# Block 0's norms on VectorE through PSUM, a GELU bias as a row of ones, a split MLP front, and heads-of-eight attention in finer parts

## The chip, the cores and the metric

One core of a Trainium2 chip. The kernel is one launch, and its time is device microseconds, the median of several runs. Engines: TensorE (PE, its weight loads PEld), VectorE (DVE), ScalarE (ACT), GpSimd (POOL), and SyncE (SP), which issues most DMAs. Each runs its own queue in order, and semaphores join them.

## What is computed

X is 16 batches of 128 tokens of 128 features, f32. Four blocks follow each other, each a gated cross-attention to a context of 77 rows and a gated feed-forward part. Blocks 0 and 2 begin with attention of 16 heads of width 8 ("heads of eight"). The feed-forward part of block 0 is itself six layers of local attention and a GELU MLP. Cut to what matters here:

```python
x = x + tanh(g_xattn[0]) * L0_xattn(layernorm(x), ctx, ctx, W1, W2, 16)   # heads of eight
x = x + tanh(g_ffn[0]) * L0_ffn(layernorm(x), ...)                        # below
...                                                                       # blocks 1, 2 (heads of eight), 3

def L0_ffn(x):                       # DEPTH 6, 16 heads of 64
    for i in range(6):
        q, k, v = split(shift_tokens(x) @ Wqkv[i])
        q, k = l2norm(q) * q_scale, l2norm(k) * k_scale    # t / max(norm, 1e-12)
        q, k = rotary(q), rotary(k)                        # with scales
        p = softmax(mask(8 * q @ k.T))                     # window of 32 and the one before
        x = (p @ v) @ Wo[i] + x
        xn = layernorm(shift_tokens(x)) * g + b
        a, gate = split(xn @ W1[i] + b1)                   # 341 + 341
        x = (a * gelu(gate)) @ W2[i] + b2 + x
```

shift_tokens moves the second half of the features by one token.

## The kernel before

X and, in block 0, Y stay in SBUF as four groups of four batches (GB 4), tokens on partitions. The order of the instructions on each engine is not the source's: the Tile framework's scheduler orders each engine's queue at build time from its own costs, keeps the data dependences, and sets the semaphores; an engine then runs its queue strictly in that order.

**Heads of eight** (`AttentionOf8`, used by `l0_xattn` and `l2_xattn`). A batch is a unit. `run` steps over n: scores of unit n (matmul L244, bias add on DVE L246, max on DVE L251, subtract on POOL L252, exp on ACT L253), row sums, reciprocal and division of unit n-1 (DVE L257, L258, POOL L259), transposes of unit n-2 (L266, copies on ACT L267), p times v of n-3 (L273, copied to oT by DVE, L275), output projection and gated add (L194) of n-4. For every four units `group` makes keys, layernorm (statistics and application on DVE, L179 to L183, power on POOL L171), transposes and queries in one go. The pool of `ps_s` has one buffer.

**Block 0's feed-forward part** (`l0_ffn`). A unit is one batch in one layer, worked in two halves of 8 heads; step k takes one half each of several units: `l0_project` (qk matmuls L454, two rotary multiplies of 128x1024 on DVE L457, squares on ACT L462, sums on DVE L463, rotary adds on POOL L466) and `l0_values` of half unit k; `l0_turn` (transposes of r, helper line L189) and `l0_scores` (mask matmul L505, scores L509, max on DVE L512, eight exps with row sums on ACT L516, reciprocal L517, division of p on POOL L518) of half unit k-3; `l0_turn_p` and `l0_mix` (L532, copy oT on ACT L534) of k-5; `l0_add` (ps_r L540, add to Y on DVE L541) of k-7. After a unit's second half, `l0_norms` makes the roots of the 32 norms of q and k:

```python
nc.scalar.activation(y, ss.bitcast(I32), AF.Exp, bias=seed, ...)   # L483: first guess
for c in (1.0 + 1.67e-4, 1.0):                                     # two Newton steps, L485 to L488, on POOL
```

and POOL multiplies r by them (L492). PSUM holds a pool "s" of two double banks (ps_qk, ps_s, ps_h) and a pool "m" of four banks for everything else. Two steps, an odd and an even one, make a pair; a half layer (8 units, two groups) is 8 pairs.

The MLP of a pair of groups hangs on fixed steps of this loop: `l0_mlp_norm` at step `at` (shift matmul ps_x L547, copies to xs, bn statistics on DVE, rs on POOL L557 to L560, adding b2 to Y on POOL L561 from the broadcast tile w_b2, four Identity activations on ACT L563), `l0_mlp_turn` at at+2, `l0_mlp_out` at at+3 and at+5 (ps_h L576 in three chunks, GELU on ACT L578, product on DVE L579 into h, w_2 matmuls L583, add to Y L584).

## Time and profile before

| | |
|---|---|
| median of 3 runs | 3260.86 us (3258.79 to 3262.26) |
| profiled execution | 3258.67 us, span 3256.9 us |
| granted TensorE clock, mean | 0.915 |
| PE busy in the span | 2756.5 us |
| first attention (heads of eight) | about 5 to 168 us |
| block 0's feed-forward part | about 168 to 2235 us |
| third block's attention (heads of eight) | about 2537 to 2700 us |

A line of a group reads: line, engine, operation, output tile <- input tiles, shapes, count, busy us, mean ns of one, idle us of the engine just before it and what ended it. A wait line reads: engine, tile and line that waited, what released it, total us, times, longest. A timeline line reads: start us, duration us, engine, line, operation, with the idle time before it in brackets. A window line: window, length, busy us and instructions of PE, PEld, DVE, ACT and POOL, granted clock, DMA share, GB/s.

### The profile page before, as it was taken

How to read it: one execution, taken by the hardware profiler on the slowest of the kernel's cores; microseconds unless marked ns; L12 is line 12 of the kernel's file. 1: busy time of each engine (PE TensorE's matmuls, PEld its weight loads, DVE VectorE, ACT ScalarE, POOL GpSimd, SP SyncE). 2: the span in 40 equal slices, each digit the busy share in tenths (PEclk: the TensorE clock that was granted, in tenths of full speed). 3: DMA queues.
4: the chain of work that ended last, by engine and by line, in shares of the span. 5: the costliest groups of instructions: out<-in, count | busy, mean ns of one | idle time of the engine just before them, and what ended most of it. 6: DMA issues, size and time to landing. Idle time of an engine off the chain costs nothing.

```text
span 3256.9 us, 50402 instructions
## 1 busy us (share of the span) xinstructions
PE 2756.5 (85%) x18912; PEld 1888.0 (58%) x18912; DVE 1876.6 (58%) x3163; ACT 1745.7 (54%) x5161; POOL 1778.9 (55%) x2030
## 2 busy tenths in 40 slices
PE   5779898989899898989898989898889678985656
PEld 4546565656566565656565656565655455653445
DVE  5566555555656564656565656545337765456553
ACT  3448676667667676758676767672222342222221
POOL 5568867686858585868776767751000451013222
PEclk8889999999999999999999999998779788997777
DMA  1020000000000000000000000002000000000003
GB/s 54 1 70 1 1 21 9 8 1 1 28 7 1 1 28 7 1 1 21 7 8 1 1 1 1 1 1 82 1 1 1 1 2 1 1 1 1 1 1 117
DMA packets 24304, 40.15 MB, mean 12 GB/s; under 512 B 1790, under 2 KB 18940, under 8 KB 22908
## 3 DMA queue, kind: packets, MB, share of 16 engines
q1 hardware_dynamic: 21036, 26.96, 2.5%
q0 software_dynamic: 2448, 9.07, 0.9%
q8 instruction: 149, 2.44, 0.3%
q10 hardware_dynamic: 576, 0.91, 0.1%
q14 instruction: 95, 0.78, 0.1%
HBM read 35.88 MB, written 1.05 MB: 11 GB/s over the span
## 4 chain that ended last, share of the span: by engine, by line
PE 46%; POOL 21%; ACT 15%; DVE 12%; issue 5%; DMA 1%; DVEq 0%; ACTq 0%; POOLq 0%
ACT p L516 7%; PE ps_t L189 7%; PE ps_qk L454 5%; POOL p L518 4%; POOL r L466 4%; PE ps_h L778 4%; POOL r L492 4%; PE ps_s L509 3%; PE ps_v L471 3%; DVE r L457 3%; PE ps_o L532 3%; PE ps_r L583 2%; PE ps_d L784 2%; PE ps_p L266 2%; PE ps_h L576 2%
## 5 line engine op out<-in xcount | busy, mean ns | idle before, releaser
L518 POOL TENSOR_TENSOR p<-p,rs 128x1024 f32<-128x1024 f32 x192 | 364.1, 1896 | 432.7 <-DVE rs L517 381.2
L516 ACT ACTIVATE p<-ps_s,mx 128x128 f32<-128x128 f32 x1536 | 539.6, 382 | 14.6 <-DVE mx L512 9.3
L457 DVE TENSOR_TENSOR r<-ps_qk,w_turn 128x1024 f32<-128x1024 f32 x384 | 454.2, 1215 | 140.2 <-PE ps_qk L454 74.8
L466 POOL TENSOR_TENSOR r<-r 128x512 f32<-128x512 f32 x384 | 480.7, 1271 | 9.5 <-DVE r L457 9.4
L454 PE MATMUL ps_qk<-w_qkv,xT 128*128 128x512 f32 x768 | 363.6, 596 | 5.3 <-ACT sq L462 3.3
L492 POOL TENSOR_TENSOR r<-r,nw_y 128x1024 f32<-128x1024 f32 x192 | 361.5, 1901 | 7.5
L516 ACT ACTIVATION_READ_ACCUMULATOR p<-ps_s,mx 128x1 f32 x1536 | 340.6, 222 | 0.0
L463 DVE TENSOR_REDUCE ss<-sq 128x16 f32<-128x1024 f32 x192 | 234.0, 1219 | 106.3 <-ACT sq L462 106.2
L189 PEld LDWEIGHTS ps_t<-const,p 128*128 128x128 f32 x1536 | 178.4, 143 | 168.8 <-ACT oT L534 110.3
L512 DVE TENSOR_REDUCE mx<-ps_s 128x8 f32<-128x1024 f32 x192 | 233.8, 1218 | 46.7 <-PE ps_s L509 46.7
L462 ACT ACTIVATE sq<-ps_qk 128x1024 f32<-128x1024 f32 x192 | 201.8, 1051 | 105.6 <-DVE r L457 103.2
L509 PEld LDWEIGHTS ps_s<-rT 64*128 64x128 f32 x3072 | 192.5, 193 | 104.1 <-ACT pT L163 49.0
L532 PEld LDWEIGHTS ps_o<-pT,v 128*64 128x64 f32 x3072 | 164.8, 137 | 122.4 <-issue 45.4
L509 PE MATMUL ps_s<-rT 64*128 64x128 f32 x3072 | 229.5, 290 | 5.8 <-ACT rT L163 5.8
L189 PE MATMUL ps_t<-const,r 128*128 128x128 f32 x1536 | 210.9, 281 | 17.2 <-POOL r L492 17.2
L471 PE MATMUL ps_v<-w_qkv,xT 128*128 128x512 f32 x384 | 224.6, 669 | 0.0
L505 PE MATMUL ps_s<-masks 128*128 128x512 bf16 x384 | 124.6, 392 | 116.8 <-ACT p L516 115.3
L473 ACT COPY v<-ps_v 128x512 f32<-128x512 f32 x192 | 114.3, 595 | 199.8 <-PE ps_v L471 199.8
L540 PEld LDWEIGHTS ps_r<-w_o,oT 128*128 128x128 f32 x1536 | 185.6, 192 | 59.5 <-issue 38.8
L189 PE MATMUL ps_t<-const,p 128*128 128x128 f32 x1536 | 212.3, 280 | 8.3 <-POOL nw_y L488 4.7
L532 PE MATMUL ps_o<-pT,v 128*64 128x128 f32 x3072 | 211.9, 279 | 1.8 <-ACT pT L163 1.2
L517 DVE RECIPROCAL rs<-rs 128x8 f32<-128x8 f32 x192 | 38.6, 201 | 300.5 <-ACT p L516 300.3
(265 smaller groups left out, 5275.9 us busy)
## 6 DMA issues: line engine op xcount, KB each, us to landing
w_qkv<-in_l_qkv SPq DMA_DIRECT2D x6, 1536.0 KB, 8.0
w_o<-in_l_o SPq DMA_DIRECT2D x6, 512.0 KB, 4.0
w<-in_l SPq DMA_DIRECT2D x6, 341.0 KB, 5.7
l_g<-in_l_g SPq DMA_DIRECT2D x1, 1152.0 KB
l_u<-in_l_u SPq DMA_DIRECT2D x1, 1152.0 KB, 11.1
l_d<-in_l_d SPq DMA_DIRECT2D x1, 1152.0 KB, 13.8
X<-in_x SPq DMA_DIRECT2D x4, 256.0 KB
l_kv<-in_l_kv SPq DMA_DIRECT2D x2, 512.0 KB, 14.4
```

What stands on the lines that cost most here:

```text
L189: nc.tensor.transpose(ps[:, j, :], in_[:, j, :], ident)
L454: nc.tensor.matmul(ps[:, a, :], lhsT=u.xT, rhs=u.w["qkv"][:, a * 1024 + g * 512 : a * 1024 + g * 512 + 512], start=True, stop=True)
L457: nc.vector.tensor_tensor(r12[:, :, a], ps[:, a].rearrange("p (h d) -> p h d", d=64).unsqueeze(1).to_broadcast([128, 2, 8, 64]), u.w["turn ...
L463: nc.vector.tensor_reduce(u.ss[:, g], sq.rearrange("p a (h d) -> p a h d", d=64), AX.X, ALU.add)
L466: nc.gpsimd.tensor_tensor(r[:, :, :, lo : lo + 32], r12[:, 0, :, :, lo : lo + 32], r12[:, 1, :, :, hi : hi + 32], ALU.add)
L471: nc.tensor.matmul(pv, lhsT=u.xT, rhs=u.w["qkv"][:, 2048 + g * 512 : 2048 + g * 512 + 512], start=True, stop=True)
L492: nc.gpsimd.tensor_tensor(r, r, y[:, g].unsqueeze(2).to_broadcast([128, 16, 64]), ALU.mult)
L509: nc.tensor.matmul(ps[:, o_, c, :], lhsT=u.rT[at, 0, c, :], rhs=u.rT[at, 1, c, :], start=False, stop=True, skip_group_check=True)
L512: nc.vector.tensor_reduce(mx, ps, AX.X, ALU.max, negate=True)
L516: nc.scalar.activation(p[:, h, :], ps[:, h, :], AF.Exp, bias=mx[:, h : h + 1], accum_out=rs[:, h : h + 1])
L518: nc.gpsimd.tensor_tensor(p, p, rs.unsqueeze(2).to_broadcast([128, 8, 128]), ALU.mult)
L532: nc.tensor.matmul(po[64 * o_ : 64 * o_ + 64, c, :], lhsT=u.v[g][:, 2 * c + o_, :], rhs=u.pT[:, 4 * o_ + c, :], start=True, stop=True)
```

## The change

Five edits, all in block 0's feed-forward part but the last.

- `l0_norms`: the clamp of the sums (POOL) and the eight Newton operations (POOL) become seven operations on DVE with y in a PSUM bank of pool "m"; the clamp becomes a minimum on the root. POOL still multiplies r by it.
- The bias b2 becomes row 85 of the third chunk of w_2; a tile `hidden`, made once and used by all layers in place of h, has ones in that row.
- `l0_mlp_norm` is split: `l0_mlp_stats` makes the statistics of both groups with one set of POOL operations at the end of step `at`; `l0_mlp_norm` (the Identities) comes at the end of at+1, the turn at at+3, the two outs at at+4 and at+6.
- The reciprocal and division of p move to `l0_divide`, called one step later.
- `AttentionOf8.run`: layernorm statistics, its application (now on ACT) with the keys, and the transposes come 3, 2 and 1 steps ahead of the group's first unit, the queries at the end of the step before it; the transposes of p go half ahead of the scores and half behind; oT is copied by ACT. `l2_xattn` adds the key bias on ACT.

```diff
+    def ln_stats(pool, in_):
+
+        st = pool.tile([128, GB, 6], F32, name="ls_st", tag="ls_st")
+        mv = pool.tile([128, GB, 2], F32, name="ls_mv", tag="ls_mv")
+        rs = pool.tile([128, 2, GB], F32, name="ls_rs", tag="ls_rs")
+        for j in range(GB):
+            nc.vector.bn_stats(st[:, j, :], in_[:, j, :])
+        for j in range(GB):
+            nc.vector.bn_aggr(mv[:, j, :], st[:, j, :])
+        nc.gpsimd.tensor_scalar_add(rs[:, 0], mv[:, :, 1], 1e-5)
+        nc.gpsimd.tensor_tensor(rs[:, 0], rs[:, 0], minus_half[:, :GB], ALU.pow)
+        nc.gpsimd.tensor_tensor(rs[:, 1], rs[:, 0], mv[:, :, 0], ALU.mult)
+        nc.gpsimd.tensor_scalar(rs[:, 1], rs[:, 1], -1.0, 0.0, ALU.mult, ALU.add)
+        return rs
+
+    def ln_apply(out_, in_, rs):
+        for j in range(GB):
+            nc.scalar.activation(out_[:, j, :], in_[:, j, :], AF.Identity, bias=rs[:, 1, j : j + 1], scale=rs[:, 0, j : j + 1])
...
-            nc.vector.tensor_copy(u.oT, po)
-
-        def out(self, u):
+            nc.scalar.copy(u.oT, po)
...
+            for n in range(-4, B + 4):
+
+                for k in (3, 2, 1):
+                    g, r = divmod(n + k, GB)
+                    if r or not 0 <= g < NG:
+                        continue
+                    if k == 3:
+                        rs[g] = ln_stats(self.pool, X[g])
+                    elif k == 2:
+                        z[g] = self.pool.tile([128, GB, 128], F32, name="z", tag="z")
+                        ln_apply(z[g], X[g], rs[g])
+                        kb = self.keys(keys(g))
+                        for j in range(GB):
+                            us[g * GB + j].kb = kb[:, :, j, :]
+                    else:
+                        ps = transposed(self.psum, z[g])
+                        zT = self.pool.tile([128, GB, 128], F32, name="zT", tag="zT")
+                        nc.scalar.copy(zT, ps)
+                if unit(n - 2):
+                    self.turned(us[n - 2], 0)
+                if unit(n):
+                    self.scores(us[n])
+                if unit(n - 2):
+                    self.turned(us[n - 2], 1)
+                if unit(n):
+                    self.exps(us[n])
+                if unit(n - 3):
+                    self.mixed(us[n - 3])
+                if unit(n - 1):
+                    self.normed(us[n - 1])
+                    us[n - 1].v = self.values(n - 1, values(n - 1))
+                if unit(n - 4):
+                    self.out(us[n - 4], n - 4, layer)
+                if unit(n + 1) and (n + 1) % GB == 0:
+                    qT = queries(zT)
                     for j in range(GB):
-                        us[n + 1 + j].qT, us[n + 1 + j].kb = ready[0][:, j, :], ready[1][:, :, j, :]
-                if 0 <= n - 2 < B:
-                    self.turned(us[n - 2])
-                if 0 <= n < B:
-                    self.scores(us[n], us[n].qT, us[n].kb)
-                if 0 <= n - 3 < B:
-                    self.mixed(us[n - 3], us[n - 3].v)
-                if 0 <= n - 1 < B:
-                    u = us[n - 1]
-                    self.normed(u)
-                    u.v = self.values(n - 1, values(n - 1))
-                if 0 <= n - 4 < B:
-                    pr = self.out(us[n - 4])
-                    gated((n - 4) // GB, (n - 4) % GB, pr, tanh_x, layer)
+                        us[n + 1 + j].qT = qT[:, j, :]
...
+            hidden = ypool.tile([128, 3, 512], F32, name="hidden", tag="hidden")
+            nc.gpsimd.memset(hidden[64:96, 2, :], 1.0)
...
-                    pair = [_Mlp(l, 2 * part + i) for i in range(2)]
-                    mlps.setdefault(at, []).extend((l0_mlp_norm, m) for m in pair)
-                    mlps.setdefault(at + 2, []).extend((l0_mlp_turn, m) for m in pair)
-                    mlps.setdefault(at + 3, []).append((l0_mlp_out, pair[0]))
-                    mlps.setdefault(at + 5, []).append((l0_mlp_out, pair[1]))
+                    pair = [_Mlp(l, 2 * part + i, hidden) for i in range(2)]
+                    mlps.setdefault((at, 1), []).append((l0_mlp_stats, pair))
+                    mlps.setdefault((at + 1, 1), []).append((l0_mlp_norm, pair))
+                    mlps.setdefault((at + 3, 0), []).append((l0_mlp_turn, pair))
+                    mlps.setdefault((at + 4, 0), []).append((l0_mlp_out, pair[:1]))
+                    mlps.setdefault((at + 6, 0), []).append((l0_mlp_out, pair[1:]))
...
+                    e, eh = half_unit(k - 4)
+                    if a and ah == 0:
+                        a.start(pool, W[a.l], xT[a.g][:, a.j, :])
+                    if b:
+                        l0_turn(pool, psum, b, bh)
+                    if a:
+                        l0_project(pool, psum, a, ah)
+                    if e:
+                        l0_divide(pool, e, eh)
+                    if d and dh == 1:
+                        l0_add(psum, d, Y[d.g][:, d.j, :])
+                    mlp_parts((k, 0))
+                    if c:
+                        l0_turn_p(pool, psum, c, ch)
+                    if b:
+                        l0_scores(pool, psum, b, bh, masks)
+                    if a:
+                        l0_values(pool, psum, a, ah)
+                    if c:
+                        l0_mix(pool, psum, c, ch)
+                    if a and ah == 1:
+                        l0_norms(pool, psum, a, seed)
+                    mlp_parts((k, 1))
...
-        w["b2"] = wpool.tile([128, 128], F32, name="w_b2", tag="w_b2")
-        nc.sync.dma_start(out=w["b2"], in_=io["l0_b2"][l : l + 1].to_broadcast([128, 128]))
+        nc.sync.dma_start(out=w["2"][85:86, 2, :], in_=io["l0_b2"][l : l + 1])
...
-    def l0_norms(pool, u, seed):
+    def l0_norms(pool, psum, u, seed):
 
         ss = u.ss.rearrange("p g a h -> p (g a h)")
-        nc.gpsimd.tensor_scalar_max(ss, ss, 1e-24)
-        y = pool.tile([128, 32], F32, name="nw_y", tag="nw_y")
+        y = psum.tile([128, 32], F32, name="nw_y", tag="m")
         t = pool.tile([128, 32], F32, name="nw_t", tag="nw_t")
+        t2 = pool.tile([128, 32], F32, name="nw_t2", tag="nw_t2")
+        rn = pool.tile([128, 2, 16], F32, name="rn", tag="rn")
 
         nc.scalar.activation(y, ss.bitcast(I32), AF.Exp, bias=seed, scale=-0.5 * float(np.log(2.0)) / 2.0**23)
         for c in (1.0 + 1.67e-4, 1.0):
-            nc.gpsimd.tensor_tensor(t, y, y, ALU.mult)
-            nc.gpsimd.tensor_tensor(t, t, ss, ALU.mult)
-            nc.gpsimd.tensor_scalar(t, t, -0.5 * c, 1.5 * c, ALU.mult, ALU.add)
-            nc.gpsimd.tensor_tensor(y, y, t, ALU.mult)
-        y = y.rearrange("p (g a) -> p g a", g=2)
+            nc.vector.tensor_tensor(t, y, ss, ALU.mult)
+            nc.vector.scalar_tensor_tensor(t2, y, -0.5 * c, t, ALU.mult, ALU.mult)
+            nc.vector.scalar_tensor_tensor(y, t2, 1.5 * c, y, ALU.add, ALU.mult)
+        nc.vector.tensor_scalar_min(rn.rearrange("p g n -> p (g n)"), y, 1e12)
         for g in range(2):
             r = u.r[g].rearrange("p a h d -> p (a h) d")
-            nc.gpsimd.tensor_tensor(r, r, y[:, g].unsqueeze(2).to_broadcast([128, 16, 64]), ALU.mult)
+            nc.gpsimd.tensor_tensor(r, r, rn[:, g].unsqueeze(2).to_broadcast([128, 16, 64]), ALU.mult)
...
-        nc.vector.reciprocal(rs, rs)
-        nc.gpsimd.tensor_tensor(p, p, rs.unsqueeze(2).to_broadcast([128, 8, 128]), ALU.mult)
         u.p.append(p)
+        u.rs = rs
+
+    def l0_divide(pool, u, g):
+        nc.vector.reciprocal(u.rs, u.rs)
+        nc.gpsimd.tensor_tensor(u.p[g], u.p[g], u.rs.unsqueeze(2).to_broadcast([128, 8, 128]), ALU.mult)
...
-    def l0_mlp_norm(pool, psum, w, Y, m):
...
+    def l0_mlp_stats(pool, psum, w, Y, ms):
+
+        st = pool.tile([128, 2, GB, 6], F32, name="ln_st2", tag="ln_st2", bufs=1)
+        mv = pool.tile([128, 2, GB, 2], F32, name="ln_mv2", tag="ln_mv2", bufs=1)
+        rs = pool.tile([128, 2, 2, GB], F32, name="ln_rs2", tag="ln_rs2", bufs=1)
+        for i, m in enumerate(ms):
+            y = Y[m.g]
+            xs = m.xs = pool.tile([128, GB, 128], F32, name="xs", tag="xs")
+            ps = psum.tile([128, GB, 64], F32, name="ps_x", tag="m")
+            nc.tensor.matmul(ps, lhsT=const_of("shift"), rhs=y[:, :, 64:128], start=True, stop=True)
+            nc.gpsimd.tensor_copy(xs[:, :, 0:64], y[:, :, 0:64])
+            nc.scalar.copy(xs[:, :, 64:128], ps)
+            for j in range(GB):
+                nc.vector.bn_stats(st[:, i, j, :], xs[:, j, :])
+                nc.vector.bn_aggr(mv[:, i, j, :], st[:, i, j, :])
+            m.rs = rs[:, :, i]
+        nc.gpsimd.tensor_scalar_add(rs[:, 0], mv[:, :, :, 1], 1e-5)
+        nc.gpsimd.tensor_tensor(rs[:, 0], rs[:, 0], minus_half[:, : 2 * GB].rearrange("p (i j) -> p i j", i=2), ALU.pow)
+        nc.gpsimd.tensor_tensor(rs[:, 1], rs[:, 0], mv[:, :, :, 0], ALU.mult)
         nc.gpsimd.tensor_scalar(rs[:, 1], rs[:, 1], -1.0, 0.0, ALU.mult, ALU.add)
-        nc.gpsimd.tensor_tensor(Y, Y, w["b2"].unsqueeze(1).to_broadcast([128, GB, 128]), ALU.add)
-        for j in range(GB):
-            nc.scalar.activation(xs[:, j, :], xs[:, j, :], AF.Identity, bias=rs[:, 1, j : j + 1], scale=rs[:, 0, j : j + 1])
-
-    def l0_mlp_turn(pool, psum, w, Y, m):
-        ps = transposed(psum, m.xs)
-        m.xT = pool.tile([128, GB, 128], F32, name="xnT", tag="xnT")
-        nc.vector.tensor_scalar(m.xT, ps, cols_of("l0_ln_g", m.l), cols_of("l0_ln_b", m.l), ALU.mult, ALU.add)
-
-    def l0_mlp_out(pool, psum, w, Y, m):
-        h = pool.tile([128, 3, 512], F32, name="h", tag="h", bufs=1)
+
+    def l0_mlp_norm(pool, psum, w, Y, ms):
+        for m in ms:
+            for j in range(GB):
+                nc.scalar.activation(m.xs[:, j, :], m.xs[:, j, :], AF.Identity, bias=m.rs[:, 1, j : j + 1], scale=m.rs[:, 0, j : j + 1])
...
+        (m,) = ms
+        h = m.hidden
...
-                nc.tensor.matmul(ps[:, j, :], lhsT=h[:n, c, j * 128 : (j + 1) * 128], rhs=w["2"][:n, c, :], start=c == 0, stop=c == 2)
-        nc.vector.tensor_add(Y, Y, ps)
+                k = n + (c == 2)
+                nc.tensor.matmul(ps[:, j, :], lhsT=h[:k, c, j * 128 : (j + 1) * 128], rhs=w["2"][:k, c, :], start=c == 0, stop=c == 2)
+        nc.vector.tensor_add(Y[m.g], Y[m.g], ps)
...
-                nc.vector.tensor_scalar_add(kT, ps, cols_of("l2_bk"))
...
+                nc.scalar.activation(kT, ps, AF.Identity, bias=cols_of("l2_bk"))
```

`_Mlp` carries the hidden tile; `in_order(f, *args)` calls f.

## The prediction

> **What bounds the kernel now.** I read the page's sums first, then the busy time by stretch, then the waits, then the timelines of two places of block 0 and one of the first attention.
>
> ```profile
> span 3256.9 us, 50402 instructions
> ...
> PE 2756.5 (85%) x18912; PEld 1888.0 (58%) x18912; DVE 1876.6 (58%) x3163; ACT 1745.7 (54%) x5161; POOL 1778.9 (55%) x2030
> ```
>
> ```profile
> 0.00:168.00 168.00, 111.60 (x1088) 83.97 (x1088) 98.32 (x151) 63.79 (x111) 86.78 (x50) 0.87 0.08 27
> 168.00:2235.00 2067.00, 1857.39 (x13401) 1248.29 (x13402) 1209.74 (x1628) 1423.53 (x4606) 1490.11 (x1816) 0.96 0.03 9
> ...
> 2537.00:2700.00 163.00, 112.70 (x1050) 85.22 (x1049) 106.28 (x169) 59.93 (x99) 85.82 (x46) 0.79 0.00 1
> ```
>
> Columns: window, its length, busy PE, PEld, DVE, ACT, POOL, clock. Block 0's FFN is the second row: PE works 1857 of 2067 us and POOL 1490, so PE leads, with 210 us of PE idle to be won. The two heads-of-eight attentions are the first and the last row: no engine is 70% busy there, so each is a chain of waits.
>
> The waits say where block 0's 210 us lie:
>
> ```profile
> POOL p L518 <- DVE rs L517: 381.2, 61, 12.0
> ...
> PE ps_s L505 <- ACT p L516: 115.3, 47, 9.4
> ...
> ACT nw_y L483 <- POOL ss L479: 114.3, 47, 4.8
> ...
> ACT xs L563 <- POOL ln_rsm L560: 74.2, 24, 5.1
> ```
>
> The second row is the one on PE: 47 waits, one of 9.4 us. The last row tells whence: the MLP's normalising on ACT waits for POOL, and the exps stand behind it in ACT's queue. One such place (POOL and ACT timelines, then windows):
>
> ```profile
> 717.48 1.90 POOL L492 TENSOR_TENSOR r<-r,nw_y 128x1024 f32<-128x1024 f32 x1
> ...
> 721.52 1.04 POOL L558 TENSOR_TENSOR ln_rsm<-ln_rsm,minus_half 128x4 f32<-128x4 f32 x1
> ```
>
> ```profile
> 723.15 1.65 ACT L563 ACTIVATE xs<-xs,ln_rsm 128x128 f32<-128x128 f32 x4 [5.13 <-POOL ln_rsm L560]
> ```
>
> ```profile
> 714.00:722.00 8.00, 2.37 (x20) 2.03 (x19) 1.35 (x2) 3.03 (x12) 7.10 (x15) 0.77 0.01 3
> 722.00:730.00 8.00, 3.76 (x10) 1.64 (x9) 1.98 (x3) 5.88 (x18) 5.27 (x6) 0.50 0.00 0
> ```
>
> POOL runs Newton steps and r*y between the two MLP groups' statistics, ACT stands, PE does 2.37 us of work in 8 and then runs at half clock. This comes once in a half layer (8 pairs of steps), 12 times in all.
>
> The steady pair, from POOL's timeline and PE's:
>
> ```profile
> 673.86 2.51 POOL L466 TENSOR_TENSOR r<-r 128x512 f32<-128x512 f32 x2
> ...
> 678.17 1.90 POOL L518 TENSOR_TENSOR p<-p,rs 128x1024 f32<-128x1024 f32 x1 [1.43 <-DVE rs L517]
> 680.02 0.24 POOL L485 TENSOR_TENSOR nw_t<-nw_y 128x32 f32<-128x32 f32 x1
> ...
> 682.60 3.76 POOL L492 TENSOR_TENSOR r<-r,nw_y 128x1024 f32<-128x1024 f32 x2
> ```
>
> ```profile
> 684.55 1.09 PE L189 MATMUL ps_t<-const,r 128*128 128x128 f32 x8 [0.48 <-POOL r L492]
> ```
>
> p, Newton, r*y, and PE's next transposes of r wait for the first r*y by 0.48 us. Pairs start at 651.26, 667.78, 684.55, 701.27: 16.5 to 16.8 us each, against 16.22 of PE work (7.22 in the odd step, call it O; 9.0 in the even one, E). So PE and POOL's chain are nearly equal bounds. The eight pairs of the half layer from 651.26 take 16.52, 16.77, 16.72, 31.68 (statistics), 27.38 and 26.79 (each with one GELU group), 17.46, 17.07: 170.4; the period over ten of them is 169.9.
>
> **The change part by part.** I wrote out each engine's queue as the changed program has it (order only) and put the trace's durations to it.
>
> *Newton on DVE.* POOL loses 8 ops per unit at a pitch of 0.32 us (680.02 to 682.60: 2.6 us) and the max (0.28, L479). DVE gains 7. The trace shows no such op; nearest are the 0.20 us reciprocal (L517) and the 0.27 us add from PSUM (L541), so 0.22 each, 1.5 in all; bounds 0.15 and 0.40, 1.1 to 2.8. DVE is 58% busy and has room for either. rn is then ready 7.4 us into E, before its reader wants it (8.7, below): free up to 0.4 us an op. y takes one of four PSUM buffers that PE also writes to, for about 2 us; the other three cover that; without them PE would stand up to 2 us a pair.
>
> *Steady pair.* POOL's new order is r-add(O), r-add(E), p(O), r*rn, p(E): p and r*rn now stand behind the even step's r-add. In E, PE runs qk first, then the masks ahead of transposes, ps_r and tp. The masks wait for exps(O), 9.53 us after O began, where PE is there at 8.94: 0.6 us, with all the rest of E's work queued behind them. From E's start: qk complete 1.97, r (two of 1.22) 4.33, r-add 6.87, p 8.72, first r*rn 10.58, next O at 10.65. Pair = 7.22 + 10.65 = 17.87 us, 1.3 longer than before, although POOL has 2.9 us less to do. If p's place were not in the chain it would be 16.2 (PE alone); if r is a further 0.9 late behind DVE's longer queue, 18.8. I take 17.9.
>
> *Statistics and normalising.* Both groups share one chain of 4 POOL ops (0.23 + 1.04 + 0.20 + 0.20) in place of two, and POOL's Y add (two of 1.27, L561) is gone. But r*rn and r-add still stand ahead of or around it: the Identities start 21.9 us into the statistics pair, and ACT's queue is now 2 Identities, v, exps(E), oT, 6 Identities, rT, so that in the next O the transposes of p wait for v until 23.2, the masks for exps until 26, the scores for rT until 29.4 and ps_o for pT until 31.4. Pairs 18.2 and 24.1, against 31.68 and a plain 16.5: the wait goes from about 15 us to about 9, in pieces of 2 to 3 us. Here the clock decides some: the trace shows 0.77 in the slice with pieces of PE work and 0.50 after the 9.4 us wait. The Trainium skill, "TensorE: Matmul & The Clock Gate", section "Why this matters for your kernels", says that only PE gaps above about 3 us drop the clock to a half; by it my pieces cost nothing and the half layer is 168.1; by the trace's 0.77, 8 us of work costs 1 to 3 us more, 170. I take the trace's: 2.
>
> *GELU groups.* They now fall on two later pairs. PE's added work is the same 8 us (three ps_h chunks of 1.75, w2 2.8); row 85 makes no matmul longer in its moving size. But the first chunk's PSUM buffer waits about 2.2 us for sq(O), ahead of it on ACT. 26.8 and 26.5 against 27.38 and 26.79. Table loads stay (23 of 1.28 us).
>
> *Bias.* The Y add was counted above. w_b's broadcast DMA (64 KB, 2.8 us to landing, once a layer) becomes one row of 512 bytes at its place in SP's queue, loaded a layer ahead: nothing; uncovered, 2.8 us in the first layer. Each GELU chunk's write into the single `hidden` tile waits for the last w2 that read it, as with h (bufs 1) before. The memset runs once on POOL beside the start.
>
> Half layer: 18.2 + 24.1 + 26.8 + 26.5 + 4 x 17.87 + 1.0 (xT's shift) + 2 (clock) = 170.1 against 169.9. Block 0: 12 x 0.2 = +2 us. Ends: steady pair 16.6 gives -61 + 2; 18.8 gives +45 + 2.
>
> *Divide moved a step later.* Its reciprocal and p are in the orders above; p(E) ends 4.3 us into the next O and is wanted only in the E after.
>
> *Heads of eight.*
>
> ```profile
> L252 POOL TENSOR_TENSOR sm<-sm,mx 128x1232 f32<-128x1232 f32 x16 | 35.9, 2247 | 35.2 <-DVE rs L258 18.6 <-DVE mx L251 10.1 <-PE ps_p L266 6.6
> ```
>
> ```profile
> 92.54 2.25 POOL L252 TENSOR_TENSOR sm<-sm,mx 128x1232 f32<-128x1232 f32 x1 [6.19 <-DVE rs L258]
> ```
>
> The subtracts of units 4 to 15 start at 56.20 and 149.83: 93.6 us for 11 units, 8.5 each. DVE's order decides: where rs of a unit follows its own max at once, subtract 2.25, exp 1.23, rs 1.43, add 1.43, reciprocal 0.24 and divide 2.25 lie in one row, about 8.8 us; where another unit's work lies between, 6.4 or 4.45. In the new order DVE also loses the oT copy (0.69 a unit) and four 0.64 z ops a group; ACT (64 of 168 us busy) takes them. By the new DVE queue the 11 steps are four such rows at the start (35), then 6.4, 4.45, 8.2 and 7.95 (partly overlapped), 8.75, 6.4, 6.4: 83.5. That is -10 in the first attention; the second has the same loop with one bias op less on DVE, I take -8. Four small POOL ops a group (0.2 + 1.04 + 0.2 + 0.2) in place of one of 1.02 cost POOL at most 0.6 x 4. Ends: -35 and +10 for both.
>
> Sum: +2 - 18 = -16 against the profiled execution's 3258.67 (span 3256.9 and 1.8 around it); that execution lies 2.2 under the median 3260.86, so the median becomes 3245.
>
> **The rivals.**
> 1. *The chain of the steady pair is not where I put it*: r*rn comes early enough and pairs stay near PE's 16.6. For it: POOL has 2.9 us less per pair, and today's pair is within 0.5 of PE's work. Against: qk, r, r-add, p, r*rn is a plain sum of measured ops in the new order. Then 48 pairs (4 in each of 12 half layers) x 1.27 = 61 us less: 3184. If the statistics wait shrinks too by half of its 9 us, 3130.
> 2. *Slower: POOL's order.* Place: r*rn behind r-add(E) and p(O), in every plain pair. It decides the sign from a pair of 17.87 + 16/48 = 18.2 us on. At 18.8, because DVE has 1.5 us more in the same stretch and r waits behind the Newton ops, it is 45 us more: 3290. For it: "POOL p <- DVE rs" is already the longest wait. Against: DVE is 58% busy.
> 3. *Nothing much moves*, the change trading one chain for another in block 0 and in the attentions alike: 3261.
>
> **How the numbers follow.** Forecast 0.42, rival 1 0.15, rival 2 0.30, rival 3 0.13. 0.2% is 6.5 us, about what a measurement of this kernel tells from no change: faster is under 3254, slower over 3267. Faster: rival 1 whole, 0.34 of the forecast's 0.42, 0.02 of rival 3: 0.5. Same: 0.05 of the forecast (its clock term up to 3 us a half layer is +12) and 0.06 of rival 3: 0.1. Slower: rival 2 whole and the rest, 0.03 + 0.05: 0.4. The range takes rival 1's 3184 and rival 2's 3290 with 10 us for the attentions' bound: 3180 to 3300; left out is rival 1's further case and what of rival 2 goes beyond, about 0.12. The forecast's own range is 3225 to 3260.
>
> **What would show it.** After: "ACT xs <- POOL ln_rsm" falls below 40 us, and the 9.4 us wait of ps_s into pieces under 4 us; plain pairs 17.9 apart with PE's transposes of r waiting 1 to 2 us for POOL; Newton ops on DVE about 0.22 us; subtract of unit 4 to 15 in about 84 us. Wrong if plain pairs are 16.2 to 16.6 (rival 1) or over 18.2 (rival 2), or if the statistics wait stays in one piece.

## The result, and the profile after

The changed kernel takes 3271.3 us (median of 6 runs, 3266.83 to 3276.79) against 3260.82 for the kernel before in the same session (6 runs, 3258.79 to 3263.98): a ratio of 1.0033, interval [1.002, 1.0046]. It is slower by 0.33%. The forecast, 3245, had the wrong sign; 3271.3 lies inside its range of 3180 to 3300, which is wide enough to hold either sign. The profiled execution took 3266.83 us. Each kernel has one profiled execution; the stage times below are read from it.

The page's sums, of the changed kernel:

```profile
span 3264.9 us, 50142 instructions
...
PE 2766.3 (85%) x18912; PEld 1891.1 (58%) x18912; DVE 1936.0 (59%) x3759; ACT 1786.9 (55%) x5229; POOL 1538.8 (47%) x1119
```

POOL lost 240 us and 911 instructions, DVE gained 59 us: the work moved as the change says. The span grew by 8.0 us all the same. Set against the kernel before at the same marks (last gated add of the first attention; last add of Y into X; the marks around the third block's attention; end), it grew thus:

| stage | before | after | difference | forecast |
|---|---|---|---|---|
| first attention, to its last add | 167.97 | 173.62 | +5.65 | -10 |
| block 0's feed-forward part, to its end | 2233.44 | 2252.24 | +13.15 | +2 |
| block 1 and what lies before the third block's attention | 2544.96 | 2562.52 | -1.24 | 0 |
| third block's attention | 2706.99 | 2718.57 | -5.98 | -8 |
| the rest, to the span's end | 3256.91 | 3264.93 | -3.56 | 0 |

The middle columns are the times of the marks, the fourth the growth within the stage. The forecast's -16 became +8.0: 15.7 us of the miss lie in the first attention and 11.2 in block 0; the other rows together take 2.8 back.

Busy time by stretch, of the first attention and block 0 (window, length, PE, PEld, DVE, ACT, POOL, clock, DMA):

```profile
0.00:168.00 168.00, 115.53 (x1000) 84.58 (x1000) 78.81 (x111) 77.08 (x140) 89.13 (x60) 0.82 0.08 27
168.00:2235.00 2067.00, 1854.97 (x13414) 1248.35 (x13413) 1301.43 (x2284) 1431.12 (x4603) 1244.94 (x881) 0.97 0.03 9
```

In block 0 POOL fell from 1490 us to 1245 in the same window, and PE's idle time stayed at 212 of 2067 (210 before; between each kernel's own marks of block 0, 213.5 of 2078.6 us and 209.6 of 2065.5). PE's waits did not shrink with POOL's load. The waits of the changed kernel:

```profile
POOL r L550 <- DVE rn L547: 304.3, 36, 10.7
...
ACT xs L628 <- POOL ln_rs L623: 82.1, 12, 7.1
...
PE ps_s L563 <- ACT p L574: 46.7, 74, 2.1
```

The first line is POOL standing idle for the root, three long times in a half layer, in the stall (the pair in which PE waits for the statistics) and the two GELU pairs; a plain pair has none of it. The third line answers to PE's wait of 9.4 us, which the kernel before has in eleven half layers: it is now in pieces of at most 2.1, as forecast. The second answers to the normalising behind POOL: it was to fall from 74 us below 40, and rose to 82. Twelve waits of about 7 us stand in place of twelve pairs of about 3 (one set of statistics for two groups in place of one each).

A plain pair, POOL's timeline and then PE's:

```profile
677.39 2.51 POOL L524 TENSOR_TENSOR r<-r 128x512 f32<-128x512 f32 x2 [3.95 <-DVE nw_t L544]
679.86 1.89 POOL L580 TENSOR_TENSOR p<-p,rs 128x1024 f32<-128x1024 f32 x1
681.71 3.76 POOL L550 TENSOR_TENSOR r<-r,rn 128x1024 f32<-128x1024 f32 x2
```

```profile
683.66 1.09 PE L211 MATMUL ps_t<-const,r 128*128 128x128 f32 x8 [1.04 <-POOL r L550]
```

This is the forecast's row: r-add(E), p(O), r*rn without a gap, and PE's transposes of r waiting for its first half, 1.04 us. O begins at 683.66, E at 690.88 and the next O at 701.76: the pair is 7.22 + 10.88 = 18.10 us; 7.22 + 10.65 = 17.87 was forecast, 16.5 to 16.8 was measured before. POOL does less and has 3.95 us of idle ahead of this row, but the row is what PE waits for.

The statistics stretch: POOL, ACT and PE, and two windows.

```profile
738.64 1.67 POOL L621 TENSOR_TENSOR ln_rs<-ln_rs,minus_half 128x8 f32<-128x8 f32 x1
740.28 1.90 POOL L580 TENSOR_TENSOR p<-p,rs 128x1024 f32<-128x1024 f32 x1
```

```profile
742.66 0.88 ACT L628 ACTIVATE xs<-xs,ln_rs 128x128 f32<-128x128 f32 x2 [7.11 <-POOL ln_rs L623]
```

```profile
744.15 1.94 PE L211 MATMUL ps_t<-const,p 128*128 128x128 f32 x8 [3.31 <-ACT v L531]
```

```profile
737.50:745.50 8.00, 4.69 (x31) 3.25 (x28) 3.52 (x4) 2.84 (x12) 6.98 (x8) 0.85 0.00 0
745.50:753.50 8.00, 6.41 (x43) 3.54 (x42) 2.65 (x5) 7.50 (x22) 2.29 (x2) 0.72 0.00 0
```

The shared power (1.67 us for 8 columns; 1.04 for 4) comes only after a root multiply that ends at 738.2, and a division of p is run between it and the rest of its own chain; so ACT waits 7.11 us, v stands behind the first two Identities, and PE waits 3.31 us for v. The clock is 0.85 and then 0.72, where it was 0.77 and 0.50.

The Newton operations on DVE were sized well: 0.185 us here, 0.22 forecast.

```profile
L544 DVE TENSOR_TENSOR nw_t<-nw_y,ss 128x32 f32<-128x32 f32 x192 | 35.5, 185 | 3.3 <-ACT nw_y L542 0.4
```

The first attention, POOL's timeline:

```profile
14.31 2.25 POOL L251 TENSOR_TENSOR kb<-khT,const 128x1232 f32<-128x1232 f32 x1 [7.06 <-ACT khT L369]
16.51 1.05 POOL L198 TENSOR_TENSOR ls_rs<-ls_rs,minus_half 128x4 f32<-128x4 f32 x1
...
107.94 2.24 POOL L251 TENSOR_TENSOR kb<-khT,const 128x1232 f32<-128x1232 f32 x1 [8.34 <-ACT khT L369]
110.14 2.25 POOL L277 TENSOR_TENSOR sm<-sm,mx 128x1232 f32<-128x1232 f32 x1
```

PE's timeline at one place of it:

```profile
97.44 1.48 PE L292 MATMUL ps_p<-const,sm 128*77 128x128 f32 x8 [1.76 <-POOL sm L284]
98.85 1.40 PE L266 MATMUL ps_s<-kb,qT 32*128 32x308 f32 x4
```

The keys' multiply kb now stands ahead of the layernorm's power in POOL's queue and waits 7.06 us for the context's keys; the power, at 7.75 us before, is at 16.51, and the first subtract at 29.83 against 24.68. At 107.94 kb stands ahead of a subtract in the same way. On PE the scores (ps_s) stand behind half of the transposes of p (ps_p), which wait 1.76 us for POOL's division.

### The profile page after: what moved, and what is told of

Same layout as the page of the kernel before. It is cut to its first block, busy times and chain, and to the rows that moved or that the text cites. A ratio compares the mean times of both kernels' runs of the same rounds, so it can differ in the third digit from the quotient of the medians.

```text
span 3264.9 us, 50142 instructions
## 1 busy us (share of the span) xinstructions
PE 2766.3 (85%) x18912; PEld 1891.1 (58%) x18912; DVE 1936.0 (59%) x3759; ACT 1786.9 (55%) x5229; POOL 1538.8 (47%) x1119
## 4 chain that ended last, share of the span: by engine, by line
PE 44%; DVE 18%; ACT 16%; POOL 15%; issue 7%; DMA 0%; DVEq 0%; ACTq 0%; POOLq 0%
ACT p L574 7%; DVE r L515 6%; PE ps_t L211 6%; PE ps_qk L512 5%; POOL r L550 4%; PE ps_h L843 4%; POOL r L524 3%; PE ps_h L643 3%; ACT sq L520 2%; PE ps_r L601 2%; PE ps_r L651 2%; PE ps_d L849 2%; PE ps_o L593 2%; PE ps_s L567 2%; POOL p L580 2%
## 5 line engine op out<-in xcount | busy, mean ns | idle before, releaser
L574 ACT ACTIVATE p<-ps_s,mx 128x128 f32<-128x128 f32 x1536 | 541.5, 385 | 86.5 <-DVE nw_t L544 70.3
L550 POOL TENSOR_TENSOR r<-r,rn 128x1024 f32<-128x1024 f32 x192 | 361.6, 1906 | 304.4 <-DVE rn L547 304.3
L512 PE MATMUL ps_qk<-w_qkv,xT 128*128 128x512 f32 x768 | 372.3, 607 | 8.3 <-ACT sq L520 6.6
L574 ACT ACTIVATION_READ_ACCUMULATOR p<-ps_s,mx 128x1 f32 x1536 | 344.4, 224 | 0.0
L211 PEld LDWEIGHTS ps_t<-const,r 128*128 128x128 f32 x1536 | 171.8, 141 | 95.5 <-POOL r L550 59.8
L166 ACT COPY pT<-ps_t 128x512 f32<-128x512 f32 x288 | 160.7, 595 | 106.0 <-PE ps_t L211 104.1
L512 PEld LDWEIGHTS ps_qk<-w_qkv,xT 128*128 128x128 f32 x768 | 131.8, 192 | 113.9 <-issue 102.4
## 6 DMA issues: line engine op xcount, KB each, us to landing
l_u<-in_l_u SPq DMA_DIRECT2D x1, 1152.0 KB, 11.4
```

The costliest lines, as they stand in the source:

```text
L211: nc.tensor.transpose(ps[:, j, :], in_[:, j, :], ident)
L512: nc.tensor.matmul(ps[:, a, :], lhsT=u.xT, rhs=u.w["qkv"][:, a * 1024 + g * 512 : a * 1024 + g * 512 + 512], start=True, stop=True)
L550: nc.gpsimd.tensor_tensor(r, r, rn[:, g].unsqueeze(2).to_broadcast([128, 16, 64]), ALU.mult)
L574: nc.scalar.activation(p[:, h, :], ps[:, h, :], AF.Exp, bias=mx[:, h : h + 1], accum_out=rs[:, h : h + 1])
```

## The experiments

A measure used throughout: the distance between the first qk matmuls of successive even steps (the median, or the lowest and highest where it varies), for the eight pairs of a half layer: three plain ones, then the one before the stall, the stall, two with GELU, the last. The period is their sum, averaged over the ten half layers that follow the first; twelve make block 0.

| kernel | the eight pairs, us | period |
|---|---|---|
| before | 16.46, 16.52, 16.52, 18.08, 30 to 31.4, 26.74, 26.79, 17.71 | 169.78 |
| after | 18.08 x 3, 18.43, 26.5 to 27.5, 27.55, 26.77, 16.74 | 170.67 |
| e2 Newton on POOL | 16.46, 16.52, 16.52, 17.6, 26.8, 28.03, 31.2, 17.47 | 170.68 |
| e3 division early | 17.05 x 3, 17.58, 25.6 to 26.5, 27.35, 26.83, 16.81 | 165.62 |
| e5 root before r-add | 16.97 x 3, 17.56, 28.3 to 30, 27.54, 26.76, 16.74 | 168.75 |
| e6 masks late too | 16.68 x 3, 17.28, 28.7 to 30.5, 27.54, 26.75, 16.73 | 167.53 |
| e7 Newton alone | 17.06 x 3, 19.52, 22.8 to 24.3, 26.24, 26.17, 16.22 | 162.93 |
| e8 split alone | 16.48, 16.55, 16.55, 17.55, 26 to 27.8, 27.76, 29.97, 17.5 | 169.39 |
| e10 Newton and bias row | 17.06 x 3, 19.52, 20.4 to 22, 26.24, 26.17, 16.22 | 160.58 |
| e11 and the two orders | 16.69 x 3, 19.31, 20.6 to 22.2, 26.23, 26.17, 16.22 | 159.91 |
| e12 and the finer second attention | 16.69 x 3, 19.31, 20.6 to 22.2, 26.23, 26.17, 16.22 | 160.06 |

**e1_attn_only.** The kernel before with `AttentionOf8` and `l2_xattn` of after; nothing of block 0's feed-forward part. The core of it:

```diff
-                if 0 <= n - 2 < B:
-                    self.turned(us[n - 2])
...
+                if unit(n - 2):
+                    self.turned(us[n - 2], 0)
+                if unit(n):
+                    self.scores(us[n])
+                if unit(n - 2):
+                    self.turned(us[n - 2], 1)
```

> The kernel before with the finer heads-of-eight attention alone; block 0's feed-forward part as before. Theory (the attention's loss lies in the attention: later start, scores queued on PE behind the first half of the transposes, which waits for POOL's division): first subtract of the first attention at about 29.8 us instead of 24.7, first attention about 5.6 us longer, second attention about 6 us shorter, block 0's pairs of steps unchanged at 16.5 us; total within 5 us of before, 3256 to 3266. Rival (the attention gains as forecast when block 0 does not follow in the same schedule): both attentions shorter by about 8 to 10 us, 3243.

3250.52 us against 3256.33: 0.9989 [0.9979, 1.0]. The third block's attention went from 162.0 to 158.4 us. In the first one the first subtract came 5.5 us later, as in after, but the last add at 167.92, level with before. So the late start need not cost anything; the +5.65 of after, which has the same source for this attention, arises where the scheduler orders it otherwise beside the changed block 0. Four more kernels below have this very source for the attention with block 0 changed, e2, e3, e5 and e6, and their last add is at 175.33, 178.18, 175.92 and 175.82: ten microseconds between kernels whose attention has the same text. The six kernels with the attention of before end it between 165.09 and 167.97. The period of block 0 stayed at 169.70.

**e2_newton_on_pool.** After, with `l0_norms` of before:

```diff
-            nc.vector.tensor_tensor(t, y, ss, ALU.mult)
-            nc.vector.scalar_tensor_tensor(t2, y, -0.5 * c, t, ALU.mult, ALU.mult)
-            nc.vector.scalar_tensor_tensor(y, t2, 1.5 * c, y, ALU.add, ALU.mult)
+            nc.gpsimd.tensor_tensor(t, y, y, ALU.mult)
+            nc.gpsimd.tensor_tensor(t, t, ss, ALU.mult)
+            nc.gpsimd.tensor_scalar(t, t, -0.5 * c, 1.5 * c, ALU.mult, ALU.add)
+            nc.gpsimd.tensor_tensor(y, y, t, ALU.mult)
```

> The changed kernel with the roots' Newton steps and clamp back on POOL, y in SBUF; all else as changed. Theory (POOL's order r-add(E), p(O), r*rn sets the plain pair's 18.1 us, and the scheduler chose it because the root comes late from DVE): POOL's order is p(O), Newton, r*y, r-add(E) again, plain pairs fall to about 16.5 us, four in each of 12 half layers, 4 x 1.6 x 12 = 75 us less, if the statistics pair does not give it back: about 3200. Rival (the later division makes the plain pair 18.1): pairs stay at 18, total 3270 or above, because POOL has 2.6 us more a pair.

3279.42 us, 1.0059 [1.0036, 1.0082], against before; the period is 170.68, as in after. Moving the Newton steps is thus worth nothing in block 0 once the other edits are there. The plain pair is back at 16.5, as expected, but the total is not the 3200 that was to follow: what the pair won went into the GELU pairs, the second above all (31.2 against 26.77). Groups of ACT's table loads in this kernel:

```profile
L645 ACT ACT_TABLE_LOAD x45 | 57.7, 1283 | 13.3 <-PE ps_h L643 12.7
...
L541 ACT ACT_TABLE_LOAD x22 | 28.2, 1283 | 0.4
```

With GELU's own 45 (23 in after), 22 at the first guess of the root and 22 at the exps of p (L574), block 0 has 89 loads against 45 in after: an exp falls between the GELU chunks and switches the table twice. The other 44 are 44 x 1.283 = 56 us of ACT.

**e3_divide_early.** After, with the division where it was:

```diff
+        nc.vector.reciprocal(rs, rs)
+        nc.gpsimd.tensor_tensor(p, p, rs.unsqueeze(2).to_broadcast([128, 8, 128]), ALU.mult)
         u.p.append(p)
...
-                    if e:
-                        l0_divide(pool, e, eh)
```

> The changed kernel with the reciprocal and the division of p back in the scores' step; Newton steps stay on DVE. Theory (the plain pair is the sum qk, r, r-add(E), p(O), r*rn): POOL's order becomes p, r-add(E), r*rn, so p's 1.86 us leave the sum and the pair falls to PE's own 16.2 to 16.6 us: 4 x 1.5 x 12 = 72 us less, about 3200. Rival (DVE's longer queue makes r late whatever POOL's order is): pairs stay at 17.5 to 18.1, total 3255 to 3275.

3217.01 us, 0.9876 [0.9858, 0.9893]. The later division alone costs 5.05 us a half layer, 57.6 us in block 0 by its marks: without it the change would have been faster. POOL's timeline of a plain pair in this kernel:

```profile
666.16 1.90 POOL L574 TENSOR_TENSOR p<-p,rs 128x1024 f32<-128x1024 f32 x1 [2.94 <-PE ps_t L211]
668.02 2.50 POOL L522 TENSOR_TENSOR r<-r 128x512 f32<-128x512 f32 x2
670.47 3.76 POOL L548 TENSOR_TENSOR r<-r,rn 128x1024 f32<-128x1024 f32 x2
```

p is ahead of the r-add, in time that POOL had idle, and r*rn follows the r-add at once: the row loses p's 1.9 us, and the plain pair 1.03, where 1.5 to 1.9 was expected. Three fifths of the 5.05 lie in the plain pairs (3.1), nearly all the rest in the stall and the pair before it.

**e4_scores_first.** After, with two calls of the attention's loop exchanged:

```diff
-                if unit(n - 2):
-                    self.turned(us[n - 2], 0)
                 if unit(n):
                     self.scores(us[n])
+                if unit(n - 2):
+                    self.turned(us[n - 2], 0)
```

> The changed kernel with one pair of calls exchanged in the heads-of-eight attention: the scores of unit n are called ahead of the first half of the transposes of unit n-2, so that they stand ahead of it in PE's queue. Theory (the scores wait behind transposes that wait for POOL's division): steps of 8.8 us between the subtracts of successive units fall to 6.4 or below, each attention 10 to 25 us shorter, block 0 unchanged: 3225 to 3250. Rival (DVE's own row of subtract, exp, sum, add sets the 8.8 us): nothing moves by over 4 us, 3271.

3260.22 us, 1.0021 [1.0006, 1.0037]: the interval overlaps after's, so the total does not separate them. In the profiled executions the stage does: the first attention ends at 169.02, 4.6 us earlier than in after, with block 0's period unchanged (170.76). The third block's attention gained nothing (156.21 us against 156.05), and the 10 to 25 us expected in each did not come. So the place of the transposes in PE's queue cost something like 4.6 us in one attention and nothing in the other; that it is this place, and not the rest of the order that the scheduler chose with it, is not shown. Five of the 15 steps still last 8.83 us, and POOL's timeline at one of them says why:

```profile
89.28 2.25 POOL L284 TENSOR_TENSOR sm<-sm,rs 128x1232 f32<-128x1232 f32 x1 [4.38 <-DVE rs L283]
91.49 2.25 POOL L277 TENSOR_TENSOR sm<-sm,mx 128x1232 f32<-128x1232 f32 x1
```

The subtract of the next unit stands behind the division of the one before, which waits for the row sums and their reciprocal: one row of subtract, exp, sum, add, reciprocal and divide in series, with 4.38 us of POOL idle. This is the rival named for this run, and the forecast's own row of about 8.8.

**e5_root_before_radd** and **e6_masks_late_too.** e5 is after with the even step's r-add queued on POOL behind r*rn; e6 also queues the even steps' masks on PE behind ps_r.

`before` is the unit before, `scaled` its r*rn, `added` the last ps_r matmul of the step.

```diff
-        for lo, hi in ((0, 32), (32, 0)):
+        with tc.issue_after(before.scaled.ins) if before is not None else contextlib.nullcontext():
+          for lo, hi in ((0, 32), (32, 0)):
...
-        for o_ in range(2):
+        with tc.issue_after(added.ins) if added is not None else contextlib.nullcontext():
+          for o_ in range(2):
```

The first half of this diff is e5, both are e6.

> The changed kernel with one order added: POOL's adds of an even step's r are queued behind the multiplications of r by the roots of the unit before (issue order alone). Theory (the plain pair's 18.1 us is the sum qk, r, r-add(E), p(O), r*rn on POOL): r-add's 2.5 us leave the sum, and r*rn then waits for the root, which DVE has at about 9.1 us after E's qk began: plain pairs 16.4 to 16.9 us, four or five in each of 12 half layers, 60 to 75 us less: 3195 to 3212. Rival (DVE's queue with the seven Newton operations sets the pair): pairs stay above 17.8, total above 3255.

> As the run with r*rn ahead of r-add(E), and in even steps the mask matmuls of the scores are queued on PE behind the output projection ps_r, as in the kernel before. Theory (once POOL's chain is shorter, PE's own wait of 0.5 us for the exps in front of the masks is on the path): plain pairs shorter by a further 0.3 to 0.6 us, 16.3 to 16.5, 15 to 30 us less than that run. Rival (the root's readiness is the bound, and PE only waits elsewhere): within 5 us of that run.

e5: 3246.26 us, 0.9948 [0.9932, 0.9965]; e6: 3228.73, 0.9894 [0.9877, 0.991]. POOL's timeline in e5:

```profile
672.11 3.76 POOL L552 TENSOR_TENSOR r<-r,rn 128x1024 f32<-128x1024 f32 x2 [0.66 <-DVE rn L549]
675.83 2.51 POOL L526 TENSOR_TENSOR r<-r 128x512 f32<-128x512 f32 x2
```

With r*rn ahead, the plain pair falls from 18.08 to 16.97, and with the masks out of the way to 16.68, near PE's own 16.2. The stall's pair grows by about 2 us in exchange, so that e5's total is well above the 3195 to 3212 that was expected. The two orders change no operation: the plain pair's 1.4 us were order, not load.

**e7_newton_alone.** Before, with the Newton steps and the clamp on DVE through PSUM (and the tile hidden in place of h, without its row of ones); the division, the MLP's front and the attentions as before.

```diff
-            nc.gpsimd.tensor_tensor(t, y, y, ALU.mult)
...
+            nc.vector.tensor_tensor(t, y, ss, ALU.mult)
...
+        nc.vector.tensor_scalar_min(rn.rearrange("p g n -> p (g n)"), y, 1e12)
```

> The kernel before (attention, divide, MLP front and bias as before; the ones row's tile stands unused) with the Newton steps on DVE through PSUM alone. POOL's order in a plain pair becomes p(O), r-add(E), r*rn, p(E), with the masks late on PE. Theory (chains of measured ops): exps(O) end, p 1.9, r-add 2.5, r*rn 1.9 gives pairs of 16.5 to 17.1; the statistics pair loses the 2.6 us of Newton between its two chains, 28 to 29 instead of 31; total 3215 to 3260. Rival (Newton on DVE is itself the loss): pairs of 18, total above 3300.

3182.15 us, 0.9762 [0.9746, 0.9779]: 6.85 us a half layer, 74.5 in block 0 by its marks. The gain is not in the plain pair, which grew from 16.5 to 17.06; it is in the stall (30 to 31.4 down to 22.8 to 24.3) and in the last pair (17.71 to 16.22). In the stall the time from the first ps_x to the Identities shortened: they run from 11.1 to 20.8 us after it before, from 8.9 to 12.4 here, and no Newton operations stand between the two groups' statistics any more. The stall fell further than the 28 to 29 expected. Twelve times the period's gain would be 82, but the first half layer has no stall to shorten (130.62 against 129.25).

**e8_split_alone.** Before, with the split front of the MLP and the bias row; Newton stays on POOL, the division at its place.

```diff
-                    mlps.setdefault(at, []).extend((l0_mlp_norm, m) for m in pair)
...
+                    mlps.setdefault((at, 1), []).append((l0_mlp_stats, pair))
+                    mlps.setdefault((at + 1, 1), []).append((l0_mlp_norm, pair))
```

> The kernel before with the MLP front in two parts and the bias row alone; Newton steps on POOL, division in the scores' step, attention as before. POOL's order in a plain pair becomes p, r-add(E), max, Newton, r*y. Theory (chains of measured ops): qk 1.9, r 2.4, r-add 2.5, max 0.3, Newton 2.6, first r*y 1.9 in one row make plain pairs of 18.5 to 19, and the statistics pair is 26 to 27 instead of 31: total 3290 to 3330. Rival (the split keeps the plain pairs at 16.5 and gains only): 3200 to 3215.

3261.9 us against 3261.57: 1.0005 [0.9996, 1.0014], no difference. The plain pairs stayed at 16.5: the sum of the new chain, 18.5 to 19, is refuted, and so is the rival of 3200 to 3215. The stall is shorter by about 4 us, and the GELU pairs take it back (27.76 and 29.97, from 26.74 and 26.79), with the same 89 table loads as e2.

**e9_keys_behind_stats.** After, with kb queued on POOL behind the layernorm's statistics:

```diff
+                        with tc.issue_after(rs[g][1].ins):
                             kb = self.keys(keys(g))
```

> The changed kernel with one order added in the heads-of-eight attention: POOL's key product kb (2.25 us) of a group is queued behind the last small operation of the next group's statistics, instead of ahead of the power of the first group's. Theory (the first attention's late start is the power waiting behind kb, which waits for the context's DMA): first subtract at about 25 us instead of 29.8, and the first attention 4 to 6 us shorter, ending near 168 to 170 us; block 0 as changed, pairs of 18.1. Rival (the start is given back later, the attention being held by its chains of 8.8 us): first subtract earlier, end within 2 us of 173.6.

3262.86 us against 3261.01: 1.0009 [1.0, 1.0019]. POOL's timeline:

```profile
8.60 2.04 POOL L198 TENSOR_TENSOR ls_rs<-ls_rs,minus_half 128x4 f32<-128x4 f32 x2
14.75 2.24 POOL L251 TENSOR_TENSOR kb<-khT,const 128x1232 f32<-128x1232 f32 x1 [3.52 <-ACT khT L370]
25.27 2.25 POOL L277 TENSOR_TENSOR sm<-sm,mx 128x1232 f32<-128x1232 f32 x1 [1.01 <-DVE mx L276]
```

The power no longer waits for the keys, the first subtract is back at 25.27 (29.83 in after), and 3.8 of those 4.6 us remain at the attention's end (169.82). This shows that kb's place in POOL's queue made the start late. Its worth at the end is 3.8 us here; in e1 the attention with the same late start ended level with before.

**e10_newton_and_bias**, **e11_and_orders**, **e12_and_second_attention.** e10 is e7 with the bias row; e11 adds the two orders of e5 and e6; e12 adds the finer attention in the third block alone, the first keeping the one before.

```diff
-        w["b2"] = wpool.tile([128, 128], F32, name="w_b2", tag="w_b2")
-        nc.sync.dma_start(out=w["b2"], in_=io["l0_b2"][l : l + 1].to_broadcast([128, 128]))
+        nc.sync.dma_start(out=w["2"][85:86, 2, :], in_=io["l0_b2"][l : l + 1])
...
-            attention = AttentionOf8(pool, psum, const_of("causal"), 8.0**-0.5, l0_w2, False)
+            attention = AttentionOf8Whole(pool, psum, const_of("causal"), 8.0**-0.5, l0_w2, False)
```

The last two lines are e12's, where `AttentionOf8Whole` is the class of before.

> The kernel before with the Newton steps on DVE and the bias as a row of ones; MLP front in one part, division in the scores' step, attention as before. Theory (the split of the MLP front is a loss once Newton is off POOL, the bias row is a gain): against the run of Newton alone, POOL loses two adds of 1.27 us in the statistics step, which stand ahead of the statistics' chains, so those two pairs are 0 to 2.5 us shorter and the half layer 160.5 to 163: 3155 to 3185. Rival (the bias row costs, the split does not): half layer at 165 or above, 3215.

> As the run with Newton on DVE and the bias row, and two orders added: r*rn ahead of r-add(E) on POOL, and the masks of even steps behind ps_r on PE. Theory (the plain pair's 17.06 us is exps(O), p(O), r-add(E), r*rn; without r-add in it the pair falls towards PE's own work): plain pairs 16.3 to 16.7, four or so in each half layer: 15 to 30 us less. Rival (the later adds of r give it back at the scores of the next unit): within 6 us of that run.

> As the run with the two orders, and the finer attention in the third block alone, the first block's as before. Theory (the second attention is 6 us shorter in the finer form in every run, since its start is not held by a DMA): second attention 5 to 7 us shorter, first and block 0 unchanged. Rival (what the second attention gains depends on the order around it): within 2 us.

e10: 3155.77 us, 0.9676 [0.966, 0.9692]; the bias row is worth 2.35 us a half layer, all of it in the stall. e11: 3152.28, 0.9668 [0.9652, 0.9684], not told apart from e10 by the total, where 15 to 30 us were expected: the plain pair went from 17.06 to 16.69, and the stall's pair grew (its mean from 21.23 to 21.84). e12: 3138.87, 0.9631 [0.9615, 0.9647], the fastest kernel of this study, 3.7% below before. Its third block's attention took 158.5 us in place of 162.5, a gain of 4.0 where 5 to 7 was expected.

The split can be read between e10 and e3, which differ in it (and in the attentions, which leave block 0's period as it is: 169.70 in e1 against 169.78, 170.76 in e4 against 170.67). Waits of e10 and then of e3:

```profile
ACT xs L600 <- POOL ln_rsm L598: 17.6, 13, 1.5
```

```profile
ACT xs L627 <- POOL ln_rs L622: 72.0, 12, 6.2
```

With Newton gone from POOL, the two groups' own chains let the Identities run from 7.5 to 11.0 us after the first ps_x; the shared chain at the end of the step stands behind r-adds and r*rn and gives them from 11.4 to 18.1. The split costs 5.04 us a half layer there.

## Why the prediction was wrong, step by step

*Block 0's sum.* Half layer forecast 170.1, measured 170.67. Counted from PE's transposes of r in the odd steps, as the forecast counted, with measured means of the ten half layers: the two statistics pairs 42.3 forecast, or 44.3 with its 2 us for the clock, 43.3 measured (17.85 and 25.49); the two GELU pairs 53.3 and 54.1; the other four with the shift of xT 72.5 and 73.2. The step "r-add(E), p(O), r*rn" was right in place and nearly in size, and e3 and e5 confirm it from two sides; what it lacks is a quarter of a microsecond ahead of the row (in the pair shown r-add starts 4.59 us into E, 4.33 forecast). The period's increase was +0.9, not +0.2, which is 7 us more over ten half layers. A term was missing: the first half layer took 132.96 us against 129.25, +3.7. It has longer plain pairs too (its last three together are 4.5 us longer) and no stall that gives this back, where the forecast had twelve half layers alike. Together they make up the 11.2 us, but for half a microsecond. So block 0's mechanism was right in the plain pair and the stall; small errors of size and the first half layer made +2 into +13.

*What the sum hid.* The forecast priced the new queues as a whole and found block 0 nearly unchanged. It was, but as the sum of terms many times as large, which the forecast did not see. Along one path of kernels, each edit put on the one before:

| edit | a half layer | block 0, by its marks |
|---|---|---|
| Newton on DVE (before to e7) | -6.85 | -74.5 |
| bias row (e7 to e10) | -2.35 | -24.9 |
| MLP front in two parts (e10 to e3) | +5.04 | +55.0 |
| division a step later (e3 to after) | +5.05 | +57.6 |

The sums are +0.89 and +13.2. From e10 to e3 the attentions change too, which alone moved block 0 by 0.1 us (before to e1). The terms depend on the path: with the other edits there, Newton's move is worth 0.0 (e2 to after), and split and bias without it -0.4 (before to e8).

*Statistics.* "The wait goes from about 15 us to about 9, in pieces": right for PE, whose longest is 3.31 us, and the Identities start 22.5 us into the statistics pair (742.66 less 720.19), 21.9 forecast. Wrong for ACT's wait: 82.1 us against below 40. The forecast took the shared chain as a saving of four operations; it laid out the chain's late place in POOL's queue, but not that ACT would stand idle for it, and it took the power as 1.04 us (1.67).

*The clock.* The forecast took 2 us from the trace's 0.77 against the rule of the Trainium skill ("TensorE: Matmul & The Clock Gate", "Why this matters for your kernels") that only gaps above about 3 us count. In the stretch shown, with one gap of 3.31 us, PE worked 4.66 us at a clock of 0.50 (from 743.14 to 749.95), so an estimate of the cost, if PE sets the time there, is half of that, 2.3 us. A gap of 3.31 does not decide between the two; e12 does. There no gap of PE is above 1.84 us in the ten half layers that follow the first, and yet:

```profile
696.64 0.38 PE L666 MATMUL ps_s<-masks 128*128 128x512 bf16 x1 [1.83 <-ACT p L677]
```

```profile
690.20:697.20 7.00, 4.32 (x25) 2.62 (x24) 4.24 (x11) 6.68 (x26) 6.58 (x8) 1.00 0.01 2
697.30:700.60 3.30, 3.30 (x9) 1.63 (x10) 1.29 (x2) 2.37 (x5) 3.20 (x3) 0.50 0.00 0
```

PE waited in pieces, the longest 1.83 us, worked 4.32 us of 7, and was then granted half the clock. So pieces under 3 us do cost clock here, and the forecast was right to follow the trace.

*GELU and bias.* "Table loads stay": right in after (45 in block 0), though e2 and e8, one or two edits away, have 89. For the bias row the forecast counted POOL's two Y adds as gone from the statistics and gave them no size of their own; they were worth -2.35 a half layer (e7 to e10), where they stood in the stall's chain.

*First attention: the step that failed.* This term, -10, came out as +5.65 and has the wrong sign. Units 4 to 15 were to take 83.5 us by DVE's queue; they took 97.7 (subtracts at 59.91 and 157.64; 93.6 before). Two things were put at nothing. First, the forecast laid out DVE and POOL and left out PE's queue, where half of the transposes stand ahead of the scores and ps_k at the end of a step: with two calls exchanged (e4) the stage ends 4.6 us earlier. Second, it costed the finer group's small POOL operations but not what they were moved past: kb, which waits for the keys of the context (PE's first ps_k starts at 12.38, when its transfer has landed), ahead of the power (e9: 4.6 us at the start, 3.8 at the end). Of the 5.65 either is most by its size; whether they add was not run. What is shown is that the late start comes from kb. The rest is in part open: the same attention ends between 167.92 and 178.18 beside different versions of block 0 (e1, e3), so that how the scheduler interleaves it decides as much as either, and no run gives a rule for it. The row of about 8.8 us that the forecast had for four of its 11 steps is there (four of them in after, five in e4); steps of 11 to 13 us, as at 97.35, where kb stood ahead of the next subtract, were not in it.

*The sign.* Put right alone, the first attention makes the forecast's sum -0.4 instead of -16; block 0 put right alone makes it -4.9. The wrong sign needed both.

*Second attention.* -8 forecast, -6.0 measured: right.

*The rivals.* The third, that one chain is traded for another and nothing much moves (3261), is nearest in total and in kind. The second had the sign; its place, the row behind r-add(E), is the one found, but the pair of 18.2 us that it asked for was not reached (18.1). The first, pairs near 16.6, is refuted.

*The last block* was costed at nothing and gave -6.4 within the -3.56 of the last row (the block before it gave +2.7). Its instructions are the same in number and order; PE's busy time there fell from 153.58 to 147.15 us at a granted clock of 0.73 and then 0.77. Why the clock differs stays open (below).

## What to carry to other kernels

Price a moved operation by the queue it lands in, on every engine whose queue changes, PE's included, and ask what it now stands ahead of or behind; a lighter engine is worth nothing if the row that others wait for gets one more link. Test the edits of a combined change one by one: here about 100 us of gain and 113 us of loss in block 0 came in one diff and looked like almost no change. An operation put at the end of a step stands behind everything that was issued in it.

## What the runs showed of the hardware

- The last block has the same instructions in the same order on PE, DVE, ACT and POOL in all fourteen kernels. Its granted clock was 0.73 in six profiled executions (before, e1, e7, e8, e10, e11; 253 us), 0.75 in e2 (249.9) and 0.77 to 0.78 in the other seven (245 to 246.6). The last block in e11 and then in e12:

```profile
2808.60:3061.70 253.10, 153.80 (x688) 109.61 (x686) 156.44 (x366) 61.88 (x109) 79.49 (x68) 0.73 0.00 1
```

```profile
2801.80:3046.90 245.10, 145.94 (x687) 105.05 (x685) 156.14 (x365) 61.97 (x109) 79.50 (x68) 0.78 0.00 1
```

  The busy times of DVE, ACT and POOL agree within 0.4 us; PE's is 8 us shorter, and so is the stage. So half of the 15.7 us between these two executions lies here, and 4.0 in the stage that was edited. The clock also moves between executions of one kernel (e1's twenty runs took 3243.68 to 3266.9 us at mean clocks of 0.921 to 0.911), so that one profile of each kernel does not tell whether an edit brought this on.
- One small exp between GELUs costs two table loads of 1.283 us. Block 0 has 45 loads in twelve of the fourteen kernels and 89 in e2 and e8, with the same activations; the order on ACT differs.
- PE's clock fell to half after pieces of waiting of at most 1.83 us (e12, 690.2 to 700.6).
- A power on POOL took 1.04 us for 128x4 and 1.67 for 128x8, while the add ahead of it took 0.23 and 0.24 (L620): the power's time grew by 0.63 us with four more columns, the add's by 0.01.
